# A four-layer graph network: the tail tiles ahead of the last pair of full tiles, a last product of its own, and stores by SyncE's queue

## The chip, the cores and the metric

The kernel runs on one core of a Trainium2 chip. The metric is the device time of one execution in microseconds (us), as the median of several runs. Besides the runs there is one execution under the hardware profiler; its span goes from the first to the last instruction on the core.

## The reference

Four graph layers follow one another on 2708 nodes with 512 features in float32. Every layer normalizes the rows of x, applies a relu to give h, and adds its output to x. Layers 0 to 2 multiply by a scaled adjacency matrix and a 512x512 weight. Layer 3, the last, is the one that the change touches:

```python
h = x @ W_sa
s_left = h @ a_sa[0, :Hd]
s_right = h @ a_sa[0, Hd:]
scores = s_left[:, None] + s_right[None, :]
e = jnp.where(adj_a != 0, jnp.exp(-jax.nn.leaky_relu(scores, 0.01)), 0.0)
attn = e / (jnp.sum(e, axis=1, keepdims=True) + 1e-05)
x_a = attn @ h
x_b = adj_b @ (x @ W_gcnb) + b_gcnb
return jax.nn.sigmoid(attn_a * x_a + attn_b * x_b)
```

Here `attn_a` and `attn_b` are one gate per row, and both adjacency matrices are the same. The layer's result is added to x, and the sum is the output.

## The kernel before, in words

The 2708 rows are split into four quarters of 677. Each quarter gives five full tiles of 128 rows, so there are 20 full tiles (numbers 0 to 19). What remains of the quarters, 32 and 5 rows of each, is gathered in two tail tiles: `NF` (20) has 4 x 32 rows, and `NF + 1` (21) has 4 x 5 rows, padded to 4 x 8. Because the quarters lie apart in memory, a store of a tail tile's result is four transfers, one for each quarter (`place`, L1232).

The last layer first works out the gates and the part `attn_b * x_b` of every tile and keeps them (`ga` on chip, `xbs` in memory). Then a loop over column strips (L1334) makes the attention weights `e` and multiplies them with h: the products of L1359 write four banks `pe`, and L1376 and L1379 divide by the row sums and write `agg`. The output then needs one more product per tile, `agg` by `W_sa`, and a closing: `result` (L1247) scales the product by the gate and adds it to the kept part (L1250, VectorE), takes a Tanh (L1253, ScalarE), adds half of it to x + 0.5 (L1254, VectorE), and stores (L1256, on POOL's queue).

Full tiles are handled two at a time. `pair_product` (L1071) makes the four half results of a pair from seven products instead of eight, after Winograd's scheme; each `part` is two matmuls of 128x128 by 128x256. Part 1 opens bank `pa`, which ScalarE copies to `v`; part 6 opens `pb`, and `u2 = v + pb`; part 2 is added to `pa`, which is then one of the four half results without any further sum. Parts 7 and 5 open `pc` and `pd`; parts 4 and 3 are added to these. The sums `u2`, `u3`, `c22`, `c21` and `c12` are made by VectorE, each from a bank and an earlier sum.

A tail tile is done by `attention` (L1258). For `NF` the product is four matmuls of 128x128 by 128x512 (L203), or, with `pieces=2`, two groups of four by 128x256. For `NF + 1` four products run side by side in groups of 32 columns (L206), ScalarE copies them (L208), and another product adds them up (L210).

After the loop over strips (L1397 on) three pairs and both tail tiles are left. Their order before is: the pair begun in the loop (tiles 14 and 15), the pair 16 and 17, tile `NF + 1`, the pair 18 and 19, tile `NF` in two pieces. Banks come from three pools: `ps_agg` has five, `ps_out` two, `ps_sm` one. `pair_bank` (L1267) takes `pb` and `pd` from `ps_sm`, the others from `ps_out`; `gates_bank` (L1113), used in the gates' stage, takes `pb` from `ps_out` and the others from `ps_agg`. The loads of x and of the kept part (`load_x`, L914) are issued on POOL's queue in the order of the tiles. A scheduler sets the final order of instructions on each engine from that of the program; each engine works through its own in order.

Of the kernel before, what the change touches and what calls it, by code (L numbers as in the profile page):

```python
# [13 lines left out]
D = 512  # L14
NC = D // P
# [8 lines left out]
NF = NQ * KT  # L24
# [13 lines left out]
def gnn_kernel(  # L38
# [20 lines left out]
    nc = tc.nc  # L59
# [57 lines left out]
    agg = big.tile([P, 2, 2, 2, 2, U * W], FP, name="agg")  # L117
# [33 lines left out]
    def new_y():  # L151
        return take(y_places)

    def load_w(w):
        w_sb = w_place[:, 0 : NC * D].rearrange("p (c o) -> p c o", c=NC)
        nc.gpsimd.dma_start(w_sb, w.rearrange("(c p) o -> p c o", p=P))
        return w_sb

    def full_cols(a, t):
        k = t % KT  # L160
        return a[..., k * P : (k + 1) * P]

    def repeat(g, n):

        while n < P:
            nc.vector.tensor_copy(g[..., n : 2 * n], g[..., 0:n])
            n *= 2

    def tile_cols(a, t, again=False):


        cs = [a[:, f, :, c] for f in range(a.shape[1]) for c in range(a.shape[3])]
        if t < NF:
            q = t // KT
            return [full_cols(c[:, q // 2, q % 2], t) for c in cs]
        o, m = (KT * P, R0) if t == NF else (KT * P + R0 - PAD, R1P)
        if a.shape[5] == R0 + R1:
            o -= KT * P
        g = new_y().rearrange("p (c n) -> p c n", c=NC)
        for c, src in enumerate(cs):  # L180
            nc.vector.tensor_copy(
                g[:, c, 0 : NQ * m].rearrange("p (i q r) -> p i q r", i=2, q=2),
                src[:, :, :, o : o + m],
            )
        n = NQ * m
        if again:
            repeat(g[:, 0 : len(cs)], n)
            n = P
        return [g[:, c, 0:n] for c in range(len(cs))]

    def tile_product(t, cs, ws):

        n = ws[0].shape[-1]

        def bank():
            return ps_out.tile([P, n], FP, tag="out", name="po")

        po = bank()  # L200
        if t <= NF:
            for c in range(NC):
                nc.tensor.matmul(po, cs[c], ws[c], start=(c == 0), stop=(c == NC - 1))  # L203
            return po
        for c in range(NC):
            nc.tensor.matmul(po[c * G : (c + 1) * G], cs[c], ws[c], start=True, stop=True)  # L206
        y = new_y()[:, 0:n]
        nc.scalar.copy(y, po)  # L208
        po = bank()
        nc.tensor.matmul(po, all_again, y, start=True, stop=True)  # L210
        return po
# [90 lines left out]
    parts = {(0, u): left[:, u * W : (u + 1) * W] for u in range(U)}  # L302
# [232 lines left out]
    def bank(name):  # L535
        return ps_agg.tile([P, W], FP, tag="agg", name=name)
# [512 lines left out]
    def weights_of_pairs(w, sums):  # L1049

        w11, w12, w21, w22 = (w[:, f : f + 2, k] for f in (0, 2) for k in range(2))
        t1, t2, t3, t4 = sums
        nc.vector.tensor_sub(t1, w12, w11)
        nc.vector.tensor_sub(t2, w22, t1)
        nc.vector.tensor_sub(t3, w22, w12)
        nc.vector.tensor_sub(t4, w21, t2)
        return {1: w11, 2: w21, 3: w22, 4: t4, 5: t1, 6: t2, 7: t3}

    def sums_of_pair(ts, places):
        (a11, a12), (a21, a22) = (  # L1060
            [full_cols(agg[:, f, t // KT // 2, :, t // KT % 2], t) for f in range(2)] for t in ts
        )
        sums_ = take(places)
        s1, s2, s3, s4 = (sums_[:, k] for k in range(4))
        nc.vector.tensor_sub(s3, a11, a21)
        nc.vector.tensor_add(s1, a21, a22)
        nc.vector.tensor_sub(s2, a22, s3)
        nc.vector.tensor_sub(s4, a12, s2)
        return {1: a11, 2: a12, 3: s4, 4: a22, 5: s1, 6: s2, 7: s3}

    def pair_product(xs_, ws, bank):  # L1071

        n = ws[1].shape[-1]

        def part(ps, k, start):
            for c in range(2):
                nc.tensor.matmul(  # L1077
                    ps, xs_[k][:, c], ws[k][:, c], start=start and c == 0, stop=c == 1,
                    skip_group_check=not start,
                )  # L1080

        def place(tag, bufs=1):
            return upool.tile([P, W], FP, tag=tag, name=tag, bufs=bufs)[:, 0:n]

        pa = bank("pa", n)
        part(pa, 1, True)
        v = place("v")
        nc.scalar.copy(v, pa)
        pb = bank("pb", n)
        part(pb, 6, True)  # L1090
        u2 = place("u2", 2)
        nc.vector.tensor_add(u2, v, pb)
        yield
        part(pa, 2, False)
        pc = bank("pc", n)
        part(pc, 7, True)
        u3 = place("u3")
        nc.vector.tensor_add(u3, u2, pc)
        yield
        pd = bank("pd", n)  # L1100
        part(pd, 5, True)
        c22 = place("s")
        nc.vector.tensor_add(c22, u3, pd)
        yield
        part(pc, 4, False)
        c21 = u3
        nc.vector.tensor_add(c21, u2, pc)
        part(pd, 3, False)
        c12 = u2
        nc.vector.tensor_add(c12, u2, pd)  # L1110
        yield [[pa, c12], [c21, c22]]

    def gates_bank(name, n):  # L1113
# [52 lines left out]
    parts = {1: range(12, 14), 7: range(14, 17), 2: range(17, 20), 4: range(20, NT)}  # L1166
# [65 lines left out]
    def place(t):  # L1232

        if t < NF:
            o = (t // KT) * Q + (t % KT) * P
            return [(0, P, o)]
        if t == NF:
            return [(q * R0, R0, q * Q + KT * P) for q in range(NQ)]
        return [(q * R1P + PAD, R1, q * Q + KT * P + R0) for q in range(NQ)]

    def loads(t):
        xt = load_x(t, xs)
        y = load_x(t, xbs)
        nc.scalar.activation(xt, xt, AF.Copy, bias=0.5)
        return xt, y

    def result(t, xt, y, parts, f):  # L1247

        for g, c in parts:
            nc.vector.scalar_tensor_tensor(  # L1250
                y[:, g], c, ga[:, t, 0:1], y[:, g], ALU.mult, ALU.add
            )
        nc.scalar.activation(y[:, f], y[:, f], AF.Tanh, scale=0.5)  # L1253
        nc.vector.scalar_tensor_tensor(xt[:, f], y[:, f], 0.5, xt[:, f], ALU.mult, ALU.add)  # L1254
        for o, m, to in place(t):
            nc.gpsimd.dma_start(out[to : to + m, f], xt[o : o + m, f])  # L1256

    def attention(t, pieces=1):  # L1258
        xt, y = loads(t)
        cs = tile_cols(agg, t)  # L1260
        n = D // pieces
        for k in range(pieces):
            f = slice(k * n, (k + 1) * n)
            pE = tile_product(t, cs, [wsa_sb[:, c, f] for c in range(NC)])
            result(t, xt, y, [(f, pE)], f)

    def pair_bank(name, n):  # L1267
        pool, tag = (ps_sm, "sm") if name in ("pb", "pd") else (ps_out, "out")
        return pool.tile([P, n], FP, tag=tag, name=name)

    def attention_of_pair(ts):

        xys = [loads(t) for t in ts]
        xs_ = sums_of_pair(ts, e_places)
        yield
        halves = [slice(k * (D // 2), (k + 1) * (D // 2)) for k in range(2)]
        for po in pair_product(xs_, ws_e, pair_bank):
            if po is not None:
                for t, (xt, y), ps in zip(ts, xys, po):
                    result(t, xt, y, list(zip(halves, ps)), slice(0, D))  # L1280
            yield
# [49 lines left out]
    wsa_sb = load_w(wsa)  # L1331
    todo = []
    summed = -1
    for n, (q, u, b) in enumerate(steps):  # L1334
        cu = slice(u * W, (u + 1) * W)
        se = ses[u]
        last = n >= len(steps) - NQ - 1
        pair = None
        if b == 0:
            pe = [ps_agg.tile([P, W], FP, tag="agg", name=f"pe{c}") for c in range(NC)]  # L1340
            m = min(W, Q - u * W)
            nc.gpsimd.dma_start(
                erow[:, 0:m], ab_rows[q, 0, u * W : u * W + m].rearrange("(o w) -> o w", o=1)
            )
            if u == 1 and q + 1 < NQ:
                lines[q + 1] = column_rows(q + 1)
        elif len(todo) >= 2 and (b == 3 if last else b in (1, 2)):
            pair = attention_of_pair([todo.pop(0), todo.pop(0)])
            next(pair)
            if last:  # L1350
                pair, last_pair = None, pair
# [35 lines left out]
        if n == 2:  # L1387
# [3 lines left out]
            ws_e = weights_of_pairs(  # L1391
                wsa_sb.rearrange("p c (k o) -> p c k o", k=2),
                [a.rearrange("p (c o) -> p c o", c=NC // 2) for a in places],
            )
# [3 lines left out]
    xt_places = [a[:, k * D : (k + 1) * D] for a in flat for k in range(3)]  # L1398
    for _ in last_pair:
        pass  # L1400
    for k in range(2):
        for _ in attention_of_pair([todo.pop(0), todo.pop(0)]):
            pass
        if k == 0:
            attention(NF + 1)
    assert not todo
    attention(NF, 2)


# [59 lines left out]
```

## Time and profile before

| what | value |
|---|---|
| median of three runs | 2078.27 us (2078.13 to 2078.53) |
| the profiled execution's own time | 2074.84 us |
| its span | 2073.0 us, 20307 instructions |
| mean granted clock of TensorE | 0.997 |
| TensorE busy (matmuls) | 2027.9 us, 98% of the span |
| VectorE busy | 1495.6 us, 72% |
| ScalarE busy | 406.1 us, 20% |
| POOL busy | 202.2 us, 10% |
| last matmul's end | 2063.87 us (in the timeline) |

Times in the profile's views count from the start of the span. Busy shares are averages over the whole span; a matmul of float32 shows as two records. POOL's busy time holds the issuing of its transfers, SyncE's transfers are listed on its queue. In the chain of waits every piece is followed back to what released it.

### The profile page before, as it was taken

The numbers are of one execution on the slowest core, as the hardware profiler recorded it, in microseconds if no ns is written. First come the engines' busy times: TensorE is split into PE (matmuls) and PEld (weight loads), VectorE is DVE, ScalarE is ACT, GpSimd is POOL, SyncE is SP. The second block draws the span as 40 slices with busy tenths as digits, with TensorE's granted clock in tenths as the row PEclk, the third lists the DMA queues.
The fourth block names the chain that finished last, engine by engine and source line by source line (L and its number), as shares of the span: only waits on it lengthen the run. The fifth ranks groups of instructions, "written<-read, shape, count | busy, mean of one in ns | idle before, by whom it ended". The sixth has DMA issues, their size and how long they took to land.

```text
span 2073.0 us, 20307 instructions
## 1 busy us (share of the span) xinstructions
PE 2027.9 (98%) x7338; PEld 1285.3 (62%) x7338; DVE 1495.6 (72%) x2593; ACT 406.1 (20%) x822; POOL 202.2 (10%) x367
## 2 busy tenths in 40 slices
PE   5999999999999999999999999999999999999998
PEld 2566655646666655666664556666677666676665
DVE  4678877756776777766587889967758876677634
ACT  1340001130000010100002130000026434444411
POOL 0111111120000011100002130001011000001012
PEclk9999999999999999999999999999999999999999
DMA  9998595555545444754454565545543333233221
GB/s 368 306 376 256 179 338 188 192 184 178 181 148 182 145 167 145 237 179 160 162 169 145 202 210 201 170 157 178 179 149 116 118 105 104 95 105 118 93 82 52
DMA packets 81332, 363.69 MB, mean 175 GB/s; under 512 B 11616, under 2 KB 16668, under 8 KB 81104
## 3 DMA queue, kind: packets, MB, share of 16 engines
q1 hardware_dynamic: 50672, 245.43, 34.5%
q0 software_dynamic: 30560, 116.97, 17.5%
q8 instruction: 58, 0.95, 0.2%
q14 instruction: 42, 0.34, 0.0%
HBM read 297.39 MB, written 62.19 MB: 173 GB/s over the span
## 4 chain that ended last, share of the span: by engine, by line
PE 88%; DVE 5%; DMA 4%; issue 1%; ACT 0%; POOL 0%; SPq 0%; POOLq 0%; DVEq 0%; ACTq 0%
PE pe L1359 17%; PE pa L541 14%; PE pc L541 14%; PE pd L541 14%; PE po L203 9%; PE pb L541 7%; PE pt L603 3%; DMA obuf<-in_yb_dram 2%; PE pd L1077 2%; PE pa L1077 2%; PE pc L1077 1%; DMA ends<-in_yt_dram 1%; PE pt L608 1%; PE pe L603 1%; PE pb L1077 1%
## 5 line engine op out<-in xcount | busy, mean ns | idle before, releaser
L1359 PE MATMUL pe<-obuf,h 128*128 128x339 f32 x1280 | 373.2, 448 | 0.0
L541 PE MATMUL pa<-obuf,h 128*128 128x339 f32 x1040 | 318.7, 451 | 2.5 <-ACT h L255 1.4
L1359 PEld LDWEIGHTS pe<-obuf,h 128*128 128x128 f32 x1280 | 241.4, 189 | 121.8 <-issue 4.1
L541 PEld LDWEIGHTS pa<-obuf,h 128*128 128x128 f32 x1040 | 196.2, 190 | 110.2 <-issue 10.3
L203 PE MATMUL po<-ends,agg 128*128 128x512 f32 x480 | 207.5, 593 | 0.0
L1225 ACT ACTIVATE e<-r,nsr 128x339 f32<-128x339 f32 x352 | 172.4, 566 | 178.2 <-DVE obuf L1229 87.1
L541 PE MATMUL pb<-t,s 128*128 128x339 f32 x560 | 171.0, 452 | 0.8 <-DVE t L513 0.8
L541 PE MATMUL pc<-t,h 128*128 128x339 f32 x560 | 169.4, 448 | 1.3 <-DVE u L588 1.3
L541 PE MATMUL pd<-t,s 128*128 128x339 f32 x560 | 169.0, 447 | 0.0
L541 PE MATMUL pd<-obuf,s 128*128 128x339 f32 x550 | 166.3, 448 | 1.1 <-DVE s L557 0.8
L575 ACT COPY v<-pa 128x339 f32<-128x339 f32 x56 | 24.7, 441 | 719.0 <-PE pa L541 693.0
L203 PEld LDWEIGHTS po<-ends,agg 128*128 128x128 f32 x480 | 90.9, 190 | 114.3 <-issue 109.5
L541 PEld LDWEIGHTS pb<-t,s 128*128 128x128 f32 x560 | 106.3, 191 | 56.1 <-DVE t L513 2.1
L541 PEld LDWEIGHTS pc<-t,h 128*128 128x128 f32 x560 | 105.8, 189 | 56.3 <-DVE u L588 2.4
L541 PEld LDWEIGHTS pd<-t,s 128*128 128x128 f32 x560 | 105.8, 189 | 54.1
L541 PEld LDWEIGHTS pd<-obuf,s 128*128 128x128 f32 x550 | 104.0, 189 | 54.8 <-DVE s L557 1.3
L541 PE MATMUL pc<-obuf,s 128*128 128x339 f32 x450 | 135.9, 448 | 0.0
L541 PEld LDWEIGHTS pc<-obuf,s 128*128 128x128 f32 x450 | 85.1, 189 | 43.8 <-issue 0.5
L935 POOL DMA_DIRECT2D xs<-ends x66 | 36.0, 545 | 780.9 <-DVE ends L934 702.2
L513 DVE TENSOR_TENSOR t<-obuf,t 128x1695 f32<-128x1695 f32 x55 | 105.2, 1913 | 0.0
L1229 DVE SCALAR_TENSOR_TENSOR obuf<-obuf,e 128x1695 f32<-128x1695 f32 x32 | 61.5, 1923 | 58.8 <-DMA obuf<-in_yb_dram 39.8
L514 DVE TENSOR_TENSOR t<-obuf,t 128x1695 f32<-128x1695 f32 x52 | 99.4, 1912 | 0.5 <-PE pc L541 0.5
(321 smaller groups left out, 2417.4 us busy)
## 6 DMA issues: line engine op xcount, KB each, us to landing
obuf<-in_yb_dram SPq DMA_DIRECT2D x132, 847.5 KB, 4.6
obuf<-osumt SPq DMA_DIRECT2D x100, 847.5 KB, 4.5
osumt<-obuf POOLq DMA_DIRECT2D x22, 847.5 KB, 12.1
xs<-ends POOLq DMA_DIRECT2D x66, 256.0 KB, 2.3
ends<-xs POOLq DMA_DIRECT2D x60, 256.0 KB, 4.1
obuf<-in_yt_dram SPq DMA_DIRECT2D x28, 339.0 KB, 3.6
obuf<-in_yb_dram POOLq DMA_DIRECT2D x11, 847.5 KB, 10.8
ends<-in_yb_dram SPq DMA_DIRECT2D x9, 847.5 KB, 9.4
```

Source lines behind the costliest of these rows:

```text
L203: nc.tensor.matmul(po, cs[c], ws[c], start=(c == 0), stop=(c == NC - 1))
L513: nc.vector.tensor_add(t2, o22, t1)
L514: at_y.append(nc.vector.tensor_add(t4, o21, t2).ins)
L541: last = nc.tensor.matmul(ps, x[:, k, :], y[:, k, :], start=start and k == 0, stop=k == KT - 1, skip_group_check=not start,)
L575: at_v.append(nc.scalar.copy(v, pa).ins)
L603: nc.tensor.matmul(ps[c], h[:, NF, c * P : (c + 1) * P], tl[:, 0, :], start=start, stop=False)
L608: nc.tensor.matmul(ps[c], h[g, NF + 1, c * P : (c + 1) * P], tl[g, 1, :], start=False, stop=True)
L935: nc.gpsimd.dma_start(xs[t], xt)
L1077: nc.tensor.matmul(ps, xs_[k][:, c], ws[k][:, c], start=start and c == 0, stop=c == 1, skip_group_check=not start,)
L1225: nc.scalar.activation(e[:, k], row, AF.Exp, bias=nsr[:, t, s : s + 1], scale=1.0)
L1229: nc.vector.scalar_tensor_tensor(b, b, 0.0, e1[:, :n], ALU.not_equal, ALU.min)
L1359: nc.tensor.matmul(pe[c], h[:, t, c * P : (c + 1) * P], a, start=(t == 0), stop=False)
```

## The change

The change does the following at the end of the program:

- Both tail tiles come between the pair 16 and 17 and the pair 18 and 19. `attention` loses its pieces: tile `NF` is one group of four products of 128x512, with four stores instead of eight.
- In the last pair `pair_product` runs part 2 as its last part (`first_block_last`). Tile 19's results are closed first, over all 512 columns; then tile 18's second half; then its first half, which is `pa` alone.
- The last pair's three stores are issued by SyncE's queue: 256 KB for tile 19 and twice 128 KB for tile 18.
- The last two pairs take their banks with `gates_bank`.

```diff
-    def pair_product(xs_, ws, bank):
+    def pair_product(xs_, ws, bank, first_block_last=False):
...
         nc.vector.tensor_add(u2, v, pb)
         yield
-        part(pa, 2, False)
+        if not first_block_last:
+            part(pa, 2, False)
         pc = bank("pc", n)
...
         nc.vector.tensor_add(c12, u2, pd)
+        if first_block_last:
+            part(pa, 2, False)
         yield [[pa, c12], [c21, c22]]
...
-    def result(t, xt, y, parts, f):
+    def result(t, xt, y, parts, f, queue=nc.gpsimd):
...
         for o, m, to in place(t):
-            nc.gpsimd.dma_start(out[to : to + m, f], xt[o : o + m, f])
-
-    def attention(t, pieces=1):
+            queue.dma_start(out[to : to + m, f], xt[o : o + m, f])
+
+    def attention(t):
         xt, y = loads(t)
-        cs = tile_cols(agg, t)
-        n = D // pieces
-        for k in range(pieces):
-            f = slice(k * n, (k + 1) * n)
-            pE = tile_product(t, cs, [wsa_sb[:, c, f] for c in range(NC)])
-            result(t, xt, y, [(f, pE)], f)
+        f = slice(0, D)
+        pE = tile_product(t, tile_cols(agg, t), [wsa_sb[:, c, f] for c in range(NC)])
+        result(t, xt, y, [(f, pE)], f)
...
-    def attention_of_pair(ts):
+    def attention_of_pair(ts, last=False, bank=None):
...
-        for po in pair_product(xs_, ws_e, pair_bank):
-            if po is not None:
+        for po in pair_product(xs_, ws_e, bank or pair_bank, last):
+            if po is not None and last:
+
+                result(ts[1], *xys[1], list(zip(halves, po[1])), slice(0, D), nc.sync)
+                for k in (1, 0):
+                    result(ts[0], *xys[0], [(halves[k], po[0][k])], halves[k], nc.sync)
+            elif po is not None:
                 for t, (xt, y), ps in zip(ts, xys, po):
                     result(t, xt, y, list(zip(halves, ps)), slice(0, D))
             yield
...
-    for k in range(2):
-        for _ in attention_of_pair([todo.pop(0), todo.pop(0)]):
+    for last in (False, True):
+        for _ in attention_of_pair([todo.pop(0), todo.pop(0)], last, gates_bank):
             pass
-        if k == 0:
+        if not last:
             attention(NF + 1)
+            attention(NF)
     assert not todo
-    attention(NF, 2)
```

## The prediction

> **What bounds the kernel now.** I read the page first: busy shares, then the chain that ended last.
>
> ```profile
> PE 2027.9 (98%) x7338; PEld 1285.3 (62%) x7338; DVE 1495.6 (72%) x2593; ACT 406.1 (20%) x822; POOL 202.2 (10%) x367
> ...
> PE 88%; DVE 5%; DMA 4%; issue 1%; ACT 0%; POOL 0%; SPq 0%; POOLq 0%; DVEq 0%; ACTq 0%
> ```
>
> TensorE bounds the whole. The diff keeps its products, though, and touches only what follows the last aggregation product, so the limit has to be read at the end. The table by stage of the last 23 us says where TensorE stops mattering (busy us of each engine, granted clock, DMA share, GB/s):
>
> ```profile
> 2050.00:2060.00 10.00, 10.00 (x46) 6.94 (x46) 8.29 (x20) 2.64 (x5) 3.17 (x7) 1.00 0.30 110
> 2060.00:2073.00 13.00, 3.87 (x18) 3.05 (x17) 4.26 (x10) 2.09 (x4) 5.07 (x10) 0.85 0.18 61
> ```
>
> TensorE is full to 2060 and has 3.87 us of the last 13; in that last stretch POOL, with its ten stores, is the longest. The chain of waits, cut to the end, says the same in order of time (start, us, what):
>
> ```profile
> 2063.66 0.44 DVE obuf L1254
> 2064.10 0.28 issue
> 2064.38 1.32 POOL out_dram L1256 x3
> 2065.70 0.18 issue
> 2065.88 1.96 POOL out_dram L1256 x4
> 2067.84 0.49 POOLq L1465
> ```
>
> From 2064.38 the end hangs on POOL issuing stores, not on arithmetic: the second half of the tail tile is finished before POOL reaches its stores. The timeline of the end:
>
> ```profile
> 2060.25 3.62 PE L203 MATMUL po<-ends 128*128 128x256 f32 x16
> ...
> 2063.08 0.56 POOL L1256 DMA_DIRECT2D out_dram<-obuf  x1 [0.23 <-DVE obuf L1254]
> ...
> 2064.38 3.95 POOL L1256 DMA_DIRECT2D out_dram<-obuf  x8 [0.74 <-DVE obuf L1254]
> ...
> 2064.96 0.43 DVE L1254 SCALAR_TENSOR_TENSOR obuf<-obuf 128x256 f32<-128x256 f32 x1 [0.48 <-ACT obuf L1253]
> ```
>
> VectorE's last result is there at 2065.39; the eighth store is issued at 2067.84 and ends at 2068.33. So POOL is 2.45 us late with it. The DMA view gives the rest (KB each, median us from issue to landing):
>
> ```profile
> out_dram<-obuf POOLq DMA_DIRECT2D x8, 32.0 KB, 1.7
> ...
> tl<-in_yt_dram SPq DMA_DIRECT2D x18, 169.5 KB, 2.5
> ...
> h<-hs SPq DMA_DIRECT2D x10, 128.0 KB, 3.7
> ```
>
> The last store lands at about 2067.84 + 1.7 = 2069.54. The span ends at 2073.0, so 3.46 us of closing work follow, which the change doesn't alter. Between span and time lie 1.84 us (2074.84 less 2073.0). The median of the runs is 3.43 us above this execution; I work out a difference in the profile and subtract it from 2078.27.
>
> **The change part by part.** TensorE's work is equal. Tile NF alone goes from two pieces of four products of 128x256 (16 matmul records, 3.62 us) to four of 128x512 (8 records). One 128x512 product costs 0.86 us in the chain (L210, two records) and a pair part of two 128x256 products also 0.86, so either form takes 4 x 0.86 = 3.44 us. The NF group moves from behind the last pair to ahead of it; part 2 of the pair moves behind parts 3 and 4. In the order of instructions TensorE now has: tail L206, pa part 1, L210, NF's four products, pb, pc, pd, pc second, pd second, pa second.
>
> On VectorE and ScalarE the counts stay too: NF's two Tanh of 256 columns (0.42 each) and two final steps (0.43) become one of each over 512 (0.63, 0.69), tile 18's one of each becomes two. The direct sums of these rows cancel; what counts is their order.
>
> Banks: the last two pairs take pb from ps_out and the others from ps_agg. On TensorE this removes waits on VectorE before the second-to-last pair's pb and pd, and before the last pair's pc. In the trace the first two aren't seen to cost anything; the third, with the neighbours pa and pb, is inside 10.94 us from pb (2052.93) to the last matmul's end (2063.87) for twelve parts of 0.86 = 10.32 and a pipeline end of 0.17: 0.45 us of stalls.
>
> After, step by step, with those rows' durations. pa part 1 starts at 2052.93 in pb's place; L210 at 2053.8 to 2053.9, since its copy by ScalarE (2053.15, 0.59) is what it needs in both kernels; NF's products from 2054.76 to 2058.19, complete at 2058.36. pb starts at 2058.19, pc 2059.05, pd 2059.92. Results are taken up 1.06 us after a part's start (pd at 2050.98, used 2052.04).
>
> VectorE works in order, and here the change adds a wait. NF's 128x512 scaling runs 2058.40 to 2059.15 (0.75, the row of the same form at 2054.96), u2 2059.25 to 2059.66. Then NF's last step stands in the queue and waits for ScalarE's Tanh (0.63) until 2059.86; it takes 0.69. Behind it waits u3, whose pc had been ready at 2060.11: it runs 2060.51 to 2060.92. TensorE waits for u3 before the second part of pc: 2060.97 instead of 2060.78, a stall of 0.19. Then c22, tile 19's scaling of the half c22, c21 (ready 2062.03) and its scaling (to 2062.97), c12 and tile 18's scaling of it (to 2063.83). pd second starts 2061.83, pa second 2062.70: ready at 2063.76. TensorE's end thus moves by about -0.1 us: hardly at all.
>
> The tail of VectorE is longer than before. Of the last pair (tiles 18 and 19), tile 19's full final step (0.69) runs 2063.75 to 2064.44, tile 18's second half (0.43) to 2064.83, and only then pa's scaling 2064.80 to 2065.28, though pa was ready a us earlier; Tanh 0.42 to 2065.71; final step to 2066.16. That is 0.77 us later than the 2065.39 of before.
>
> Stores. POOL loses ten stores (two of 256 KB, eight of 32 KB, 0.56 and 0.49 us each) and gets four of 64 KB for NF from 2060.55, past by about 2062.6 and landed by 2065: off the path. Its loads of NF move ahead of those of tiles 18 and 19; all twelve such loads are issued by 2024.7 and land some 3.4 us later, while tile 19's are first used at 2061; I cost this at nothing, and they would have to be 30 us late to show. SyncE gets three stores and its queue is idle from 1991, so nothing is queued behind its wait on VectorE; its first two go at 2064.5 and 2064.9 and the last at about 2066.2, against 2067.84. So 1.64 us of issue time are gained, and the remaining question is landing.
>
> No SyncE store to memory is in this trace. Below: 1.7 us, the POOL store of 32 KB. Above: 3.7, SyncE's 128 KB loads, made under heavy traffic. The nearest quiet row is SyncE's 169.5 KB load, 2.5 as a median and 2.2 at least; the last store has 128 KB, and before it 384 KB are moved out in time. I take 2.2. The Trainium skill has a rule here (DMA: Bandwidth & Descriptors, Anatomy of one DMA): a fixed 2.0 us, mostly the write's receipt, plus bytes over 436 GB/s. That makes 2.3 for this store; its section on latency gives SyncE's queue some 0.4 us less to the first byte, so 1.9. For the measured 32 KB POOL store the rule makes 2.08 where the row has 1.7, so it is some 0.4 too dear. By the rule as it stands the sum below is -1.0, with the queue's advantage -1.4. The same page (Issuing engines are not separate DMA queues) speaks against much from a change of queue: it saves only the issuing time, as usually small beside the transfer. Here 3.95 us of issue are at the very end, so the saving counts, but it can't be larger than that.
>
> Sum: last issue 2067.84 to 2066.2, -1.64; landing 1.7 to 2.2, +0.5; together -1.14, span 2071.9, own time 2073.7, median 2078.27 - 1.1 = 2077.2. This is 0.05%, far under the 0.2% (4.2 us) that a measurement of this kernel can tell from no change.
>
> **The rivals.**
>
> 1. VectorE doesn't hold up the end: the NF wait falls away and the last scaling follows pa directly. The last issue is then at about 2065.2 (2063.8 + 0.48 + 0.42 + 0.43 and gaps): -2.1 us, 2076.1. Against it is the fixed order on VectorE, with 1.12 us of final steps ahead of the last scaling.
>
> 2. Slower: SyncE's store lands late. Its price is the landing time above 2.2, its place the last 128 KB store. From 3.34 us on, the change loses; at the 3.7 of the loads under traffic, +0.4 us, 2078.6. Against it: DMA is idle at that time but for these stores (share 0.18). To lose over 0.2% the landing would have to be 7.5 us, which no quiet row shows.
>
> 3. The change does nothing on time: the longer VectorE tail (another 0.5 us from waits I don't see) eats most of the saved issues, -0.3 us or less, 2078.0.
>
> **How the numbers follow.** The forecast (-0.5 to -1.7 us) 0.58; rival 1 and beyond (-1.7 to -3) 0.14; rival 3 0.13; rival 2 0.15. The sum's own range is 2076.5 to 2077.8; with rival 1 below, the landing of 3.7 above and 0.3 us for the median's spread, 2075.9 to 2078.9. Faster by over 0.2% needs more than 4.2 us, but all that stands between the last result and the last landing is 4.15 us: 0.03. Slower by over 0.2% needs a landing nobody shows or a stall on the moved group: 0.05. Within: 0.92.
>
> **What would show it.** Profile after: ten POOL stores gone from the end; NF's four POOL stores near 2060.6; VectorE's last step at 2065.7 to 2066.2; last SyncE issue near 2066.2 and a landing of 2 to 2.5 us; a TensorE gap of about 0.2 us before the second part of pc; 3.4 to 3.5 us from last landing to the span's end. Wrong would be: a last landing after 2069.5, a closing part that has grown with SyncE's stores in it, or any shift before 2052, where I expect none.

## The result and the profile after

| | before | after |
|---|---|---|
| median of 20 runs each, us | 2077.57 (2073.54 to 2083.37) | 2073.19 (2070.55 to 2078.56) |
| the profiled execution: own time, span, us | 2074.84, 2073.0 | 2070.74, 2069.0 |

The ratio of the times is 0.9981, with a 95% interval of 0.9974 to 0.9989: some 3.9 us less (2.3 to 5.4). The forecast of -1.1 us had the sign and not the size; the measured time lies under its range.

With 20 runs each kernel spreads over 8 to 10 us, far more than any step at the end of the program. The profiles show why the end can still be read: they shift against each other before the last strip, and repeat each other after it. I therefore count from the start of the last product for the row sums (`pse` in the chain, L1375, L1380 after), which all kernels share, to the end of the span, and call this the closing stretch. It is 37.72 us before (2035.28 to 2073.0) and 33.55 us after (2035.45 to 2069.0): -4.17 us, which agrees with the times. How exact that is: by the timelines, from `pse` to the first product of tile `NF + 1` (L206) it takes 16.82 or 16.83 us in all ten kernels of this document that share the order up to there. What varies more is the landing of the last stores, by some 0.3 us (below).

The page and the table by stage after (busy us of each engine, granted clock, DMA share, GB/s):

```profile
PE 2028.0 (98%) x7330; PEld 1282.2 (62%) x7330; DVE 1495.6 (72%) x2592; ACT 406.2 (20%) x822; POOL 198.8 (10%) x361
...
2050.00:2060.00 10.00, 10.00 (x40) 5.71 (x39) 7.20 (x17) 3.27 (x6) 3.35 (x7) 1.00 0.30 110
2060.00:2069.00 9.00, 3.96 (x18) 2.84 (x16) 5.42 (x12) 1.46 (x3) 2.01 (x4) 0.89 0.30 89
```

TensorE's work is the same. In the last stretch POOL has 2.01 us instead of 5.07, and VectorE, with 5.42, is now the engine with most to do. The timeline of the end and the DMA view (KB each, median us to landing):

```profile
2061.01 2.01 POOL L1259 DMA_DIRECT2D out_dram<-obuf  x4 [1.43 <-DVE obuf L1257]
2061.10 0.73 PEld L1077 LDWEIGHTS pc<-obuf,agg 128*128 128x128 f32 x4 [0.37 <-DVE u L1099]
...
2064.71 1.97 SPq L1259 DMA_DIRECT2D out_dram<-obuf  x3
2064.93 0.48 DVE L1253 SCALAR_TENSOR_TENSOR obuf<-pa,ga,obuf 128x256 f32<-128x256 f32 x1
...
2065.89 0.43 DVE L1257 SCALAR_TENSOR_TENSOR obuf<-obuf 128x256 f32<-128x256 f32 x1 [0.48 <-ACT obuf L1256]
```

```profile
out_dram<-obuf SPq DMA_DIRECT2D x1, 256.0 KB, 2.0
out_dram<-obuf SPq DMA_DIRECT2D x2, 128.0 KB, 1.9
```

The last store alone, in the window 2066 to 2067:

```profile
out_dram<-obuf SPq DMA_DIRECT2D x1, 128.0 KB, 1.7
```

VectorE ends at 2066.32, and SyncE's last store, of 128 KB, lands 1.7 us after its issue. All this is close to the working ahead of the result. What was not looked at there are the rows of L1465 (L1470 after), the `with tile.TileContext` around the whole program, with which every engine closes its queue. These are its rows before, from 2060 to 2072.3 (queue, instruction, count, ns least/median/most, first and last start), and with them SyncE's waits from 2030 on (us in total, times, longest):

```profile
L1465 SPq EVENT_SEMAPHORE  x9: 28/28/1777, 2067.6 to 2069.9; - x9
L1465 SPq DRAIN  x2: 7/7/7, 2069.9 to 2070.0; - x2
L1465 PEldq DRAIN  x1: 3833/3833/3833, 2060.1 to 2060.1; - x1
L1465 ACTq DRAIN  x1: 444/444/444, 2064.5 to 2064.5; - x1
L1465 DVEq DRAIN  x1: 466/466/466, 2065.0 to 2065.0; - x1
L1465 POOLq DRAIN  x1: 4717/4717/4717, 2067.5 to 2067.5; - x1
...
SPq L1465 <- DMA out_dram<-obuf: 78.2, 2, 76.5
SPq L1465 <- PEq L1465: 2.9, 2, 2.4
```

And after:

```profile
L1470 SPq DRAIN  x2: 7/7/7, 2068.1 to 2068.2; - x2
L1470 POOLq DRAIN  x1: 4103/4103/4103, 2062.3 to 2062.3; - x1
...
SPq L1470 <- DMA out_dram<-obuf: 0.9, 1, 0.9
SPq L1470 <- PEq L1470: 0.7, 2, 0.5
```

These drain rows begin while their engine is still at work. ScalarE's ends at 2064.94 and VectorE's at 2065.47, within 0.1 us of their last instructions (2064.94 and 2065.39). POOL's goes from 2067.5 to 2072.2, though its last store was issued by 2068.33: 3.9 us go by after POOL's last work. SyncE, which waits for the stores, had all landings at 2069.9 and then waited 2.4 us for the others. The row names TensorE's queue, but TensorE had closed at 2063.9; the one still open was POOL's. After the change POOL's drain is over at 2066.4, ahead of SyncE's 2068.1, and what follows SyncE's last landing shrinks from 3.1 us to 0.9.

### The profile page after: what moved, and what is told of

Read it like the earlier page. It is cut to its first block, busy times and chain, and to the rows that moved or that the text cites. A ratio compares the mean times of both kernels' runs of the same rounds, so it can differ in the third digit from the quotient of the medians.

```text
span 2069.0 us, 20285 instructions
## 1 busy us (share of the span) xinstructions
PE 2028.0 (98%) x7330; PEld 1282.2 (62%) x7330; DVE 1495.6 (72%) x2592; ACT 406.2 (20%) x822; POOL 198.8 (10%) x361
## 4 chain that ended last, share of the span: by engine, by line
PE 83%; DVE 7%; DMA 5%; issue 4%; POOL 1%; ACT 0%; SPq 0%; POOLq 0%; DVEq 0%; ACTq 0%
PE pe L1364 17%; PE pc L541 13%; PE pa L541 13%; PE pd L541 13%; PE po L203 8%; PE pb L541 7%; PE pt L603 3%; DMA obuf<-in_yb_dram 3%; PE pd L1077 1%; PE pc L1077 1%; PE pa L1077 1%; PE pt L608 1%; PE pe L603 1%; DMA osumt<-ends 1%; DVE ends L1004 1%
```

## The experiments

The theory to test: POOL's queue closes 3 to 4 us after POOL's last work, and in the kernel before this drain, not the last landing, set the end. The rival is the account of the forecast: issue and landing alone, with a closing part that stays as it is. Every kernel has one profile, and the stretches are read from it; in the times, each interval overlaps that of the changed kernel.

**The queue alone.** The kernel before, with only tile `NF`'s eight stores issued by SyncE (`result` gets a `queue` argument, as in the change):

```diff
-            result(t, xt, y, [(f, pE)], f)
+            result(t, xt, y, [(f, pE)], f, nc.gpsimd if pieces == 1 else nc.sync)
```

> The kernel before, with one edit: the eight stores of tile NF's two halves are issued by SyncE instead of POOL. Order, pairs and banks stay. I read the stretch from the last row-sum product (pse) to the span's end: 37.72 us before (2035.28 to 2073.0), 33.55 us after (2035.45 to 2069.0). Theory (drain): after its last transfer POOL's queue runs a closing drain, 2067.5 to 2072.2 before and 2062.3 to 2066.4 after, and the end can't come sooner. POOL's last issue is now tile 19's store, done at about 2063.6, its drain over at about 2067.5; SyncE's last store lands near 2068.5; stretch 34.1 us, -3.6 us against before. Rival (issue and landing only, closing part always 3.46 us): last landing 2069.54 to 2068.5, stretch 36.7, -1.0 us.

Its closing stretch is 34.69 us (2035.51 to 2070.2), -3.03 against before; the ratio to before is 0.9981 (0.9973 to 0.9988). SyncE's eight stores, POOL's drain row and SyncE's wait in it:

```profile
2064.35 3.60 SPq L1256 DMA_DIRECT2D out_dram<-obuf  x8
...
L1465 POOLq DRAIN  x1: 3793/3793/3793, 2063.3 to 2063.3; - x1
...
SPq L1465 <- PEq L1465: 0.7, 2, 0.5
```

POOL's drain ends at 2067.1; SyncE closes at 2069.4 and no longer waits for POOL. Eight stores moved to another queue, with the order, the products and the banks of before, are worth three quarters of the gain. That is the theory's side (-3.6), far from the rival's (-1.0); the interval of the times, -2.5 to -5.6 us, leaves the rival out too. The missing 0.6 us is SyncE's own: its last landing came at 2069.4, where 2068.5, and 0.23 us for the later `pse`, were reckoned. Issue and landing explain little: the eight stores take SyncE 3.60 us to issue and 1.6 to land, against 3.95 and 1.7 on POOL. The last landing comes 0.73 us earlier in the stretch, and what follows it falls from 3.1 to 0.8 us.

**The stores back to POOL.** The changed kernel, with `nc.sync` left out of the last pair's three `result` calls:

```diff
-                result(ts[1], *xys[1], list(zip(halves, po[1])), slice(0, D), nc.sync)
+                result(ts[1], *xys[1], list(zip(halves, po[1])), slice(0, D))
...
-                    result(ts[0], *xys[0], [(halves[k], po[0][k])], halves[k], nc.sync)
+                    result(ts[0], *xys[0], [(halves[k], po[0][k])], halves[k])
```

> The changed kernel, with the last pair's three stores issued by POOL again. Everything else of the change stays. Drain theory: POOL's last issue ends near 2066.9, the drain some 3.5 to 4 us later at 2070.5 to 2070.9, stretch from the last pse to the end 36.0 to 36.4 us, +2.5 to +2.9 against the changed kernel, so most of the gain is gone. Rival: only issue and landing count, 0.2 us more issue and 0.5 us more landing: stretch 34.2, +0.7 us.

The stretch is 36.15 us (2034.25 to 2070.4), +2.60 against the changed kernel, as the theory had it and far from the rival's +0.7. The ratio to before is 0.9995 (0.9987 to 1.0003), not told apart from no change.

```profile
2065.41 0.54 POOL L1259 DMA_DIRECT2D out_dram<-obuf  x1 [0.52 <-DVE obuf L1257]
...
L1470 POOLq DRAIN  x1: 4188/4188/4188, 2065.4 to 2065.4; - x1
...
SPq L1470 <- PEq L1470: 2.6, 2, 2.1
```

The last landing is seen by SyncE at 2067.6, the drain ends at 2069.6, and SyncE waits 2.1 us between them. Without the queue, the change of order, product and banks is worth 1.57 us of the stretch (37.72 to 36.15): with three stores at the end in place of eight, POOL's last work ends 1.35 us earlier in it (31.70 for 33.05), and the drain is over 3.65 us later instead of 3.87.

**One store of three.** Only tile 19's store, which lands before the last one, goes back to POOL:

```diff
-                result(ts[1], *xys[1], list(zip(halves, po[1])), slice(0, D), nc.sync)
+                result(ts[1], *xys[1], list(zip(halves, po[1])), slice(0, D))
```

> The changed kernel, with only tile 19's 256 KB store (the first of the last three, ready at 2064.68) issued by POOL; the two later ones stay with SyncE. Drain theory: POOL's issue ends near 2065.3, the drain at 2069.0 to 2069.3, past the landing of SyncE's last store (2068.1): stretch 34.5 to 34.8 us, +0.9 to +1.3 against the changed kernel. Rival: tile 19's store still lands at 2067.1, before SyncE's last: 0.

The stretch is 34.30 us (2036.30 to 2070.6), +0.75 against the changed kernel, just under the theory's +0.9 and not the rival's 0.

```profile
L1470 POOLq DRAIN  x1: 4057/4057/4057, 2065.8 to 2065.8; - x1
...
SPq L1470 <- PEq L1470: 1.4, 2, 0.9
```

SyncE closes at 2069.1 and waits 0.9 us until POOL's drain is over at 2069.9. A store that nobody waits for still sets the end, since it is the last thing that POOL does. In the times (ratio 0.9978, 0.9970 to 0.9985) 0.75 us is under the noise.

**What the drain belongs to.** The changed kernel, with one late instruction of POOL that moves nothing off the chip:

```diff
                     result(ts[0], *xys[0], [(halves[k], po[0][k])], halves[k], nc.sync)
+                nc.gpsimd.memset(xys[0][1][:, halves[0]], 0.0)
```

> The changed kernel, with one POOL instruction on the chip added at the very end: a memset of tile 18's spent scratch (128x256), which waits for VectorE's last step at 2066.3. No transfer is added. Does the drain belong to POOL's transfers or to any late work of POOL? If to transfers: POOL is busy for under 1 us more, its drain follows at once since its transfers were done at 2064.4, stretch 33.5 to 34 us, 0 to +0.4 against the changed kernel. If to any late instruction: drain of 3.5 to 4 us from 2066.8, stretch 36 us, +2.5.

The side of the transfers was wrong. The stretch is 35.41 us (2041.89 to 2077.3), +1.86; the ratio to before 0.9987 (0.9981 to 0.9994).

```profile
2072.81 0.31 POOL L1283 MEMSET obuf<- 128x256 f32 x1 [3.36 <-DVE obuf L1257]
...
L1471 POOLq DRAIN  x1: 3725/3725/3725, 2072.8 to 2072.8; - x1
...
SPq L1471 <- PEq L1471: 2.6, 2, 2.1
```

The memset is over at 2073.12, POOL had issued its last transfer 3.4 us before the memset began (64 KB, 1.9 us to land), and the drain ends at 2076.5: 3.4 us after an instruction that only writes on chip. So it is not the transfers that are waited for; the drain follows POOL's last work of either kind. The +2.5 of the other side was too much: the drain was over 3.4 us after the memset, where 3.5 to 4 us were reckoned, and the memset itself a little earlier than reckoned.

**The last product of its own.** The changed kernel, with part 2 of the last pair in its old place:

```diff
-        for po in pair_product(xs_, ws_e, bank or pair_bank, last):
+        for po in pair_product(xs_, ws_e, bank or pair_bank):
```

> The changed kernel, with part 2 of the last pair back in its old place, right after pb; order, banks and SyncE's stores stay. What is the last product of its own worth? Theory: the end is set by VectorE's queue, not by the last product. pa is ready early and its scaling and closing run between other steps; the last product is then pd's, ready near 2064.0 (times as in the changed kernel's trace), c12 and its scaling end near 2064.95, tile 19's closing near 2065.6, tile 18's half near 2066.0 against 2066.3: stretch from the last pse to the end 33.2 to 33.3 us, -0.3 against the changed kernel. Rival: the reorder is what brings the gain, since one sum fewer follows the last product: stretch longer than 33.55, by 0.4 us (c12 0.42).

The stretch is 33.18 us (2037.52 to 2070.7), -0.37: the number is the theory's, the way to it only in part. VectorE's last step ends 30.18 us after `pse`, against 30.87 in the changed kernel: -0.69, where -0.3 was reckoned. SyncE's last landing follows it after 2.2 us instead of 1.8, so more than half of that is lost again: its last two stores now go out one right behind the other, and the last lands in 2.0 us instead of 1.7. The reordered part, meant to save a sum at the end, thus costs 0.7 us on VectorE and about 0.4 of the stretch, since `pa`'s scaling then stands last in VectorE's queue. This kernel and the next ran once each, so they have no ratio of times.

**The old banks.** The changed kernel, with `gates_bank` left out for the last two pairs:

```diff
-        for _ in attention_of_pair([todo.pop(0), todo.pop(0)], last, gates_bank):
+        for _ in attention_of_pair([todo.pop(0), todo.pop(0)], last):
```

> The changed kernel, with the old banks: the last two pairs take pb and pd from the pool of one and the others from the pool of two. Theory: the banks bring nothing, since the waits they remove were hardly seen in the trace before (0.31 us at most before one product): stretch 33.5 to 33.9 us. Rival: with both tail tiles in the same two banks, pa and pc of the last pair wait for tile NF's scaling, some 0.5 to 1 us of TensorE: stretch 34.1 to 34.6.

33.66 us (2044.04 to 2077.7), +0.11, inside the theory's range, but not for its reason. The edit changed more than the banks: TensorE's order is another one.

```profile
2067.96 0.73 PEld L1077 LDWEIGHTS pc<-obuf 128*128 128x128 f32 x4 [0.38 <-DVE obuf L1253]
...
2068.94 1.08 PE L1077 MATMUL pa<-ends,agg 128*128 128x256 f32 x4
...
2071.59 1.02 PE L1077 MATMUL pd<-ends,obuf 128*128 128x256 f32 x4
```

Part 2 (the second `pa`) runs right behind `pc`'s first part here, as in the kernel before, and the last product is `pd`'s, as in the run just shown. So what the reordering costs is saved, and something else is lost. Against that run, which has the new banks and the same two last products, the stretch is 0.48 us longer and TensorE's last matmul ends 0.31 later; `pc`'s first weights wait again for tile `NF`'s scaling (0.38). The new banks are thus worth some 0.5 us where the last products are alike, and in the changed kernel the reordered part takes about 0.4 of it back. That the two cancel is a reading across two runs; why the scheduler moved part 2, the record doesn't show.

**VectorE's last steps reordered.** In the changed kernel, all scalings of the last pair come first, each with its Tanh, and then the closing steps with their stores (`scaled`, `tanh` and `closed` are the pieces of `result`):

```diff
...
+                for f, c in zip(halves, po[1]):
+                    scaled(t1, y1, f, c)
+                tanh(y1, slice(0, D))
+                for k in (1, 0):
+                    scaled(t0, y0, halves[k], po[0][k])
+                    tanh(y0, halves[k])
+                closed(t1, x1, y1, slice(0, D))
+                for k in (1, 0):
+                    closed(t0, x0, y0, halves[k])
```

> The changed kernel, with another order of the last closing steps on VectorE: pa's scaling goes right behind c12's, ahead of the closing steps of tile 19 and of tile 18's second half, and the Tanh of each follows its scaling. Stores and products stay. Theory (VectorE's queue sets when the last store is issued, POOL's drain is past): last closing step ends near 2065.85 instead of 2066.32, stretch 33.1 us, -0.45 against the changed kernel. Rival (something else, a landing or a drain, ends last): 33.5, no change.

33.37 us (2037.83 to 2071.2), -0.18: neither side. VectorE's last step does come 0.57 us earlier (30.30 us after `pse`), but SyncE closes only 0.18 earlier (32.47 against 32.65). Its three stores are now issued within 1.3 us; the last one waits some 0.2 us for the issue of the one ahead of it and lands in 1.9 us instead of 1.7. What VectorE gave was lost behind the stores. The time's ratio to before is 0.9986 (0.9976 to 0.9996).

**Both tail tiles earlier.** The same, with the tail tiles ahead of both last pairs:

```diff
+    attention(NF + 1)
+    attention(NF)
     for last in (False, True):
         for _ in attention_of_pair([todo.pop(0), todo.pop(0)], last, gates_bank):
             pass
-        if not last:
-            attention(NF + 1)
-            attention(NF)
```

> As the kernel with pa's scaling first, and both tail tiles also ahead of the second-to-last pair, so that only pairs are left at the end. POOL's last stores are then those of tiles 16 and 17, near 2060.5. Theory: POOL's drain is over near 2065, before SyncE's last landing, and the end stays with VectorE's last steps: stretch 32.7 to 33.3 us. Rival (drain): if POOL's stores slip past 2063 its drain ends after 2067.5 and sets the end: above 33.6.

33.16 us (2037.94 to 2071.1), -0.39; ratio 0.9980 (0.9971 to 0.9990). POOL's drain ends at 2067.2, ahead of SyncE at 2070.2, so the theory's side holds.

**POOL out of the end altogether.** The changed kernel, with all 15 stores after the strip loop issued by SyncE:

```diff
-            queue.dma_start(out[to : to + m, f], xt[o : o + m, f])
+            (queue or at_close[0]).dma_start(out[to : to + m, f], xt[o : o + m, f])
...
+    at_close[0] = nc.sync
     for _ in last_pair:
```

> The changed kernel, with every store after the strip loop (the three pairs and both tail tiles, 15 stores) issued by SyncE, so that POOL's last work is the last load at about 2024.7 us. Theory: POOL's closing drain goes wherever POOL's work ends: it starts near 2025, takes 3 to 4 us there and costs nothing; the end stays with the last SyncE store, stretch from the last pse to the end 33.4 to 33.8 us, no change against the changed kernel's 33.55. Rival: the drain is tied to the program's end or to SyncE's landings, or SyncE's fuller queue holds up the last stores: 34 us or more.

33.83 us (2035.57 to 2069.4), +0.28; ratio 0.9983 (0.9972 to 0.9994).

```profile
2024.45 0.54 POOL L916 DMA_DIRECT2D obuf<-xbs  x1
...
L1473 POOLq DRAIN  x1: 4711/4711/4711, 2024.4 to 2024.4; - x1
...
SPq L1473 <- PEq L1473: 0.7, 2, 0.5
```

The drain is there, 4.1 us after POOL's last load, forty us ahead of the end, and costs nothing. It belongs to the end of POOL's work and not to that of the program. Relieving POOL further brings nothing; SyncE's closing came 0.28 us later instead, with VectorE's last step where it was (30.87 us after `pse`). A single profile doesn't tell whether the longer queue is the cause: in the four kernels with this same order on VectorE and the same last store (after, one store by POOL, late memset, this one) SyncE has all landings 1.8 to 2.1 us after VectorE's last step. Steps of 0.3 us and less, -0.18 and +0.11 above too, are therefore not told apart.

**Put together.** The product order of old, the tail tiles ahead of both pairs, all closing stores by SyncE.

> What the runs point to, put together: both tail tiles ahead of the last two pairs, part 2 of the last pair in its old place, every store after the strip loop by SyncE. Theory: only VectorE's last steps and one landing remain: stretch 32.9 to 33.2 us, -0.4 to -0.6 against the changed kernel and -4.6 against the kernel before, whose time falls by 0.2 to 0.25%. Rival: the steps that gained alone overlap: 33.2 to 33.6.

33.46 us (2034.64 to 2068.1), -0.09; ratio 0.9982 (0.9972 to 0.9993). The rival's side: the small gains don't add up. VectorE's last step is as early as with part 2 in place (30.14 us after `pse`), but SyncE closes 2.4 us behind it. Of the kernels tried, the shortest stretches (33.16 and 33.18) are 0.4 us under the changed kernel's; the times of such kernels can't be told apart from its own.

In all twelve profiles the stretch is the later of the end of POOL's drain and of SyncE's last landing, and then 0.7 to 0.9 us to the end. In the four where the drain is the later, SyncE's wait ends within 0.2 us of it; in the five that the table leaves out, SyncE's landing is the later. The later of the two is in bold. Times in us from each span's start:

| kernel | POOL's last work ends | its drain ends | SyncE has all landings | span's end | closing stretch |
|---|---|---|---|---|---|
| before | 2068.33 | **2072.2** | 2069.9 | 2073.0 | 37.72 |
| after | 2063.02 | 2066.4 | **2068.1** | 2069.0 | 33.55 |
| NF's stores by SyncE | 2063.87 | 2067.1 | **2069.4** | 2070.2 | 34.69 |
| last stores by POOL | 2065.95 | **2069.6** | 2067.6 | 2070.4 | 36.15 |
| one store by POOL | 2066.39 | **2069.9** | 2069.1 | 2070.6 | 34.30 |
| late memset | 2073.12 | **2076.5** | 2074.6 | 2077.3 | 35.41 |
| all closing stores by SyncE | 2024.99 | 2029.1 | **2068.5** | 2069.4 | 33.83 |

## Why the prediction was right or wrong

- **TensorE: right.** Its end was to move by -0.1 us. In the closing stretch it is 28.59 us before (2063.87 less 2035.28) and 28.51 after (2063.96 less 2035.45). The stall before pc's second part was put at 0.19 us; it is there, with u3 as its cause: the weights wait 0.37 us, and the matmul starts 0.13 us later than one part (0.86) behind pd's (2061.10 against 2060.11).
- **VectorE's longer tail: right.** The last step was to end at 2066.16; it ends at 2066.32, and the whole end lies 0.17 later in this profile. This order costs 0.6 to 0.7 us on VectorE; part 2 in its old place or an earlier scaling gives it back there, and 0.2 to 0.4 us of it in the stretch.
- **POOL's moved loads and the banks.** No wait for the moved loads is seen at the end, as forecast. The waits that the banks remove were put inside 0.45 us of stalls of TensorE; against the run with the same last products the old banks cost 0.48 us. The run with the old banks differs from the changed kernel by only 0.11 us, but its product order changed too.
- **The landing: mis-sized on the careful side.** SyncE's last 128 KB store was taken at 2.2 us and takes 1.7; the other one takes 2.0. The estimate from the Trainium skill (DMA: Bandwidth & Descriptors, Anatomy of one DMA, less the queue's shorter way to the first byte) was 1.9, between the two, and -1.4 for the sum. Before, all landings were seen at 2069.9, not 2069.54.
- **The step that failed** is "The span ends at 2073.0, so 3.46 us of closing work follow, which the change doesn't alter." It was not a constant. It held a wait for POOL's drain, which the change takes off the end. In the stretch, SyncE's last landing moves by -1.97 us (34.62 to 32.65) where -1.14 was forecast: 0.36 because the landings before were seen later than reckoned, 0.3 because SyncE's last landing came earlier (2068.1 for 2068.4), 0.17 from the shift between the profiles. What follows it goes from 3.1 to 0.9 us, -2.2, where 0 was forecast. Together -4.17.
- **The chain that misled.** The chain of waits before ends with POOL's stores and a short piece on POOL's queue at L1465, at 2068.33. That is 4.7 us ahead of the span's end, and the chain shows nothing of those. I read the stores as the bound and their landing as the end, and took SyncE's 2.4 us of waiting at that line for fixed work. The row was in the view of waits, and the drain in the rows of L1465. With the drain, taken as 3.9 us behind POOL's last work as before, the forecast would have read: SyncE's last landing at 2066.2 + 2.2 = 2068.4, 0.8 us to the end, span 2069.2.
- **The queue's worth.** The rule that the prediction cites, that a change of queue saves issuing time only, is not what this case shows. The queue alone is worth 3.03 us, but the issuing of the eight stores shrank by just 0.35 (3.95 to 3.60). Of the 3.03, 2.3 fell behind the last landing, where POOL's drain was, which the rule does not count.
- **The bound for a large gain was wrong for the same reason.** The 4.15 us from the last result to the last landing were called all that could be saved; with the drain 6.8 us lay behind VectorE's last result (2065.39 to 2072.2), and 0.03 for more than 0.2% was far too little for a result of about 0.2%.
- **The rivals.** The slower one, a late landing of SyncE's store, didn't come (1.7 to 2.0 us). VectorE falling away didn't come, nor did the third, that the change does nothing. What did come was not among them; of the signs named, 3.4 to 3.5 us from the last landing to the end is the one that failed (0.9).

## What to carry to other kernels

Read the rows of the line that closes the program (here that of the `with tile.TileContext`) before calling anything behind the last landing fixed: see when each engine's queue has closed and what the last waiter waits for. Give the last stores to a queue that closes quickly, and let the one that closes slowly end its work some us earlier; here, one store or even one memset on POOL at the end cost 0.75 to 1.86 us, while stores of POOL that were issued 5.1 us ahead of SyncE's last landing (2063.02 and 2068.1) cost nothing. A product or a sum saved at the end is worth little when another engine's queue, in its fixed order, stands behind it.

## What the runs showed of the hardware

POOL's closing drain ended 3.2 to 4.2 us after its last work in every kernel, after transfers and after a memset alike, where ScalarE's and VectorE's ended within 0.1 us of theirs before and after. What POOL does in that time no row shows, and it wasn't tried on other work than transfers and one memset. SyncE's last store, of 128 KB, landed 1.7 us after its issue where its queue had issued nothing for some 0.8 us before it (after, one store by POOL, late memset), and 1.9 to 2.0 us after it right behind another store (part 2 in its old place, old banks, scalings first, both tail tiles earlier, put together).
